# Two sparse graph-attention layers: denominators summed into rows, masks read earlier, 17 targets summed early instead of 13

## The chip, the core and the metric

The kernel runs on one core of a Trainium2 chip: TensorE (PE) for products, VectorE (DVE), ScalarE (ACT) and GpSimd (POOL) for elementwise work, and DMA queues, most of them issued by SyncE (SP) and, for gathers, by GpSimd. The metric is the device time of one execution in microseconds (us). Before the change the median of three runs is 1807.55 us (1801.66 to 1808.13).

## The reference

There are N = 3327 nodes with 1024 features, an adjacency matrix (int32, symmetric, ones on its diagonal, some 17 ones in a row), and two layers. Each adds an attention over the neighbours to its input and normalizes the sum. Everything is f32.

```
# layer 0, eight heads of 128
h     = (x @ W0).reshape(N, 8, 128)
e     = leaky_relu(a_src·h_i + a_dst·h_j, 0.2), -inf where adj == 0
x     = layernorm(x + softmax_j(e) @ h)
# layer 1, one head
h     = x @ W1
e     = leaky_relu(h_i·a1 + h_j·a2, 0.2), excluded where adj == 0
x     = layernorm(x + relu(softmax_j(e) @ h))
```

The exponential of a leaky ReLU of a sum is written as the larger of two products of exponentials, so an edge weight is `max(r_i * u_j, v_j)` with one factor r per target and head and two numbers u, v per source and head. These 16 numbers stand behind the 1024 columns of h in each row of the table `h0_d` (1040 columns in use). A softmax is a weighted sum of rows of h divided by a sum of weights, the denominator.

## The kernel before, in words

Nodes are handled as 26 tiles of 128. A tile as the rows that are summed into is called a target here. The kernel has three stages.

**Projection** (from L743 on). For each tile: load x, transpose it on TensorE (`flip`), multiply by W0 in three column cuts of eight products each (`project`, L546), copy the result out of PSUM on ScalarE (`keep`, L565) and store it to `h0_d`. Two PSUM banks take the cuts in turn. Between every second product `pace` runs other work, one step of a Python generator at a time, so the order of all queues is written out by hand:

- *Lists.* Which edges a target has is found from its rows of adj. `load_mask` reads 128 rows by a GpSimd DMA that turns int32 into bytes, into one of three buffers (L535). `clear` takes the diagonal out (GpSimd). `words` counts the ones of each half on ScalarE (L350, two passes and their accumulators), makes `deg_b` (L352) and packs the bytes to words on DVE. `ends` and `ends2` turn counts into places with a product (L366, L391) and a string of small GpSimd operations. `keys`, `columns`, `ways`, `places`, `spread`, `give`, `take` and `sources` then pick the columns of the ones (DVE), move them to their places by products (TensorE), and leave indices `idx`, target numbers `tgt` and row factors `re_d`. The generator `listing` does this for one list after the other; a mask is counted in its last step for the list four ahead, so masks are read evenly over the projection.
- *Early sums.* Sources in the first half of the nodes (tiles 0 to 12) are complete at half time. From tile 13 on, `sums_so_far` adds up what targets 0 to EARLY - 1 receive from them: EARLY is 13. Per target it gathers two blocks of 4 x 128 rows (L641), makes weights and their products with the marks of the targets (L659, L662), sums by TensorE (L671), and stores a partial row block `half_d` and partial denominators `dens`.

**Layer 0, edges** (`sparse`, class `Layer0`, driven by `pipeline`). A target has up to five blocks: 0 and 1 with sources from the first half, 2 and 3 from all nodes, and a last one of 128 places. A target that was summed early has only the last three. Each block of 4 x 128 rows is gathered by four indirect DMAs (L1033) into one of five buffers; its buffer is free again when its products are done. `weights` makes the weights in PSUM (`way`, L1109 and L1110), copies them to SBUF (L1112, ScalarE), and multiplies them into marks (L1114, DVE, 1024 columns). `sums` then multiplies 128 x 32 pieces of that by 128 x 128 pieces of the rows, so that four groups of 32 targets go to four quarters of the output (L1145). The target's own row is scaled by its weight (`own`: L1092 on ScalarE for late targets, L1088 on DVE with the partial row added for early ones) and enters by a product with the identity (L1126).

The denominator of a block is one product with the weights of four groups and eight heads as the 32 stationary columns and the marks as 128 moving columns (L1155, L1138). That gives all 32 x 128 combinations, so `finish` masks the ones that belong together (`met`, L1167, with the constant `meets`) and adds them up with a second product (L1168, with `heads`). The early sums do the same (L719, L707, L737). Then come the division, the residual, the norm, and the stores for layer 1.

`pipeline` says with `plans` how many steps of the finishing of the previous targets run after each block. Targets alternate: a late one, then an early one.

**Layer 1, edges** (class `Target`): per target the same gathers from `y_d`, products in three cuts (L1257), then the projection by W1 (L1289) and the norm.

```
            def finish(self):

                met = sbuf("met", [NG * H, P], 2)
                nc.vector.tensor_tensor(met, self.den[: NG * H, :P], meets, OP.mult)
                nc.tensor.matmul(self.den[:, P:], met, heads, start=True, stop=True)
                yield
```

Of the kernel before, what the change touches and what calls it, by code (L numbers as in the profile page):

```python
# [9 lines left out]
F32 = mybir.dt.float32  # L10
# [16 lines left out]
def kernel(  # L27
# [57 lines left out]
    EARLY = NTH  # L85
# [35 lines left out]
    cnt = const.tile([P, NT, 4], F32, name="cnt")  # L121
# [10 lines left out]
    meets = const.tile([NG * H, P], F32, name="meets")  # L132
    heads = const.tile([NG * H, H], F32, name="heads")
# [181 lines left out]
    class Edges:  # L315
# [6 lines left out]
        def __init__(self, ph, t):  # L322
            self.ph, self.t = ph, t
            self.d, self.deg, self.end2 = cnt[:, t, :2], cnt[:, t, 2:3], cnt[:, t, 3:]
# [18 lines left out]
        def words(self, ad, junk):  # L343
# [7 lines left out]
            self.deg_b = sbuf("deg_b", [P, 2], 4, dt=BF16)  # L351
            nc.scalar.activation(self.deg_b, self.d, AF.Copy)  # L352
            w = ad.bitcast(I32)
            for n in range(3):
                m = WD >> n
                half = sbuf(f"wd{n}", [P, m], 4 if n == 2 else 1, dt=I32)
# [6 lines left out]
        def ends(self, tri_b):  # L363
# [4 lines left out]
            end, off, low, high = (v[:, n : n + 2] for n in (0, 2, 4, 6))  # L368
            self.mid, self.over, self.offs = v[:, 8:10], v[:, 10:12], v[:, 12:14]
            self.more, self.mid2, self.start, self.off2 = (v[:, n : n + 1] for n in range(14, 18))  # L370
# [5 lines left out]
            nc.gpsimd.tensor_scalar(high, end, float(HG2), None, op0=OP.max)  # L376
            nc.gpsimd.tensor_tensor(self.over, high, low, OP.subtract)
            nc.gpsimd.tensor_tensor(self.more, self.over[:, :1], self.over[:, 1:], OP.add)
            nc.gpsimd.tensor_copy(self.more_b, self.more)
            nc.gpsimd.tensor_tensor(self.deg, self.d[:, :1], self.d[:, 1:], OP.add)  # L380
            nc.gpsimd.tensor_copy(self.offs, off)
            nc.gpsimd.tensor_tensor(self.offs[:, :1], off[:, :1], self.d[:, 1:], OP.subtract)
            nc.gpsimd.tensor_tensor(self.offs[:, :1], self.offs[:, :1], self.over[:, :1], OP.subtract)
            mv = self.ph.mvs[self.t % 4][:, :, : XB + 1 : XB]
            nc.gpsimd.tensor_copy(mv[:, 0, :], self.offs)
            nc.gpsimd.tensor_tensor(mv[:, 1, :], self.offs, mv[:, 0, :], OP.subtract)

        def ends2(self, all_b):
# [6 lines left out]
            nc.gpsimd.tensor_tensor(self.off2, self.start, self.d[:, 1:], OP.subtract)  # L395
            nc.gpsimd.tensor_tensor(self.off2, self.off2, self.over[:, 1:], OP.add)
# [117 lines left out]
    with ExitStack() as own, tc.manual_schedule():  # L514
        ph = Phase(own, "proj", {"A": 2, "T": 1})
        pool, bank = ph.pool, ph.bank
        part = Phase(own, "part", {})
        opening = ExitStack()
# [35 lines left out]
        def keep(t, c):  # L554
            if t not in hts:
                hts[t] = ph.sbuf("ht", [P, HW0], 3)
            ht, acc, c0 = hts[t], accs.pop((t, c)), CUTS0[c]
            m = min(CUTS0[c + 1], D) - c0
            if c == 2:
                nc.scalar.activation(sd0[:, t].rearrange("p a h -> p (a h)"), acc[:, m:], AF.Copy)  # L560
                lists[t].factors()
# [13 lines left out]
        def count(t):  # L575
            if t < NT:
                clear(t)
                lists[t].words(ads.pop(t), junk)
                if t:
                    load_mask(t + 2)  # L580

        def listing():

            for t in range(-1, NT):
                old, new = lists[t] if t >= 0 else None, lists[t + 1] if t + 1 < NT else None
                for s in range(4):
# [4 lines left out]
                    if s == 1 and 2 < t + 3 < NT:  # L591
                        lists[t + 3].ends(tri_b)
                    if s == 2 and t >= 0:
                        clear(t + 4)
                    if s == 3 and 2 < t + 3 < NT:
                        lists[t + 3].ends2(all_b)
                    yield
# [4 lines left out]
                if new:  # L602
                    new.ways()
                yield
                if old:
                    old.sources()
                    yield
                while new and t + 1 not in scored:
# [5 lines left out]
                count(t + 4)  # L614
                yield

        scored, cleared, kept, soon = set(), set(), {}, []
        steps, slots, done = listing(), [0, 0], [0]

        def pace():  # L620

            slots[0] += 1
            while done[0] * slots[1] < slots[0] * (8 * (NT + 1)):
# [5 lines left out]
        def sums_so_far():  # L629

            part.more_banks(own, "part", {"L": 1})
            src = [near[1], part.pool.tile([P, NG, HG], F32, bufs=1, name="far"), near[0]]
# [60 lines left out]
            owed = None  # L693
            for s in range(EARLY):
                acc = part.bank("L", [P, 2, 4, DH], "part")
                made = []
                for b in range(HB):
# [7 lines left out]
                    if b == 0 and owed:  # L705
# [851 lines left out]
```

## Time and profile before

| what | value |
|---|---|
| median of three runs | 1807.55 us |
| the profiled execution | 1883.75 us, span 1882.0 |
| granted TensorE clock, mean | 0.923 |
| busy: PE, PE weight load | 1637.2 us (87%), 934.7 (50%) |
| busy: DVE, ACT, POOL | 1184.3 us (63%), 514.0 (27%), 1105.5 (59%) |
| DMA | 586.89 MB, 312 GB/s in the mean |
| queue of the gathers and masks (software) | 457.74 MB, 69.9% of the 16 engines' span |
| queue of plain transfers (hardware) | 126.52 MB, 18.3% |
| projection, layer 0, layer 1 | about 0 to 585, 585 to 1190, 1190 to 1882 us |

A group line reads: source line, engine, operation, output and inputs, shapes, count; busy time and mean of one; idle time of the engine just before it and what ended that. A line of waits has the waiting engine and line, what it waited for, the total in us, how often, and the longest. "issue" is idle time for which the profile shows no cause. The profiled execution is longer than the runs of the median, so shares and durations are read from it and its sums are made against its own time.

### The profile page before, as it was taken

To read this page: it belongs to the slowest core of one execution; us is meant where nothing else is said; L and a number is where in the kernel's file an instruction comes from. 1 tells how busy PE (TensorE), PEld (TensorE's weight loads), DVE (VectorE), ACT (ScalarE), POOL (GpSimd) and SP (SyncE) were. 2 spreads that over 40 slices of the span, in tenths; PEclk is the share of its full clock that TensorE was granted. 3 is DMA by queue.
4 is the path that set the end of the run, shared out by engine and by line. 5 is a ranking of instruction groups with operands and counts; after the bars stand their busy time and mean duration, and the time that the engine had idled before them with its cause. 6 is when DMAs were issued, how large, how long until landed. Compare 5 with 4: busy or idle time off the path is not lost.

```text
span 1882.0 us, 35565 instructions
## 1 busy us (share of the span) xinstructions
PE 1637.2 (87%) x13168; PEld 934.7 (50%) x13168; DVE 1184.3 (63%) x3262; ACT 514.0 (27%) x1519; POOL 1105.5 (59%) x1580
## 2 busy tenths in 40 slices
PE   8899899999995777778677767499999999999998
PEld 4566565565663555545454544234444444444443
DVE  5799998887755777777677786334444444444343
ACT  5666554444431222222222222011111110111110
POOL 4533356666645666666666556466666666666650
PEclk9999999999996778788888877799999999999999
DMA  7566869888779999999999999799999999999990
GB/s 184 90 136 117 149 173 261 230 273 248 272 245 348 390 403 372 374 380 389 380 394 395 363 366 328 267 369 389 385 379 373 389 390 385 369 385 377 369 355 34
DMA packets 187319, 586.89 MB, mean 312 GB/s; under 512 B 36641, under 2 KB 46651, under 8 KB 187136
## 3 DMA queue, kind: packets, MB, share of 16 engines
q0 software_dynamic: 131056, 457.74, 69.9%
q1 hardware_dynamic: 55922, 126.52, 18.3%
q8 instruction: 107, 1.75, 0.4%
q14 instruction: 76, 0.62, 0.1%
q10 hardware_dynamic: 158, 0.26, 0.0%
HBM read 587.80 MB, written 51.23 MB: 340 GB/s over the span
## 4 chain that ended last, share of the span: by engine, by line
PE 64%; DVE 14%; issue 9%; ACT 5%; DMA 5%; POOL 2%; another core or an unknown queue 0%; SPq 0%; DVEq 0%; ACTq 0%; POOLq 0%
PE mm L1289 20%; PE acc L1257 14%; PE mm L546 10%; PE acc L1145 9%; PE part L671 3%; PE acc L1126 2%; PE tr L197 2%; PE acc L1134 2%; ACT junk L350 1%; ACT own L1092 1%; DVE e L1114 1%; DMA wt<-in_L_gnn_W_dram 1%; DMA src<-h_d,idx 1%; DVE top L309 1%; DVE y L1177 1%
## 5 line engine op out<-in xcount | busy, mean ns | idle before, releaser
L546 PE MATMUL mm<-wt,xT 128*128 128x347 f32 (+1 forms) x1248 | 413.6, 473 | 4.6 <-DMA wt<-in_L_gnn_W_dram 4.2
L1289 PE MATMUL mm<-wt,xT 128*128 128x512 f32 x832 | 387.9, 605 | 0.1
L1033 POOL DMA_INDIRECT src<-y_d,idx x256 | 258.8, 1011 | 145.4 <-issue 56.6
L546 PEld LDWEIGHTS mm<-wt,xT 128*128 128x128 f32 x1248 | 227.3, 193 | 122.5 <-issue 23.9
L1033 POOL DMA_INDIRECT src<-h_d,idx x184 | 200.9, 1092 | 123.3 <-PE den L1155 34.4
L1289 PEld LDWEIGHTS mm<-wt,xT 128*128 128x128 f32 x832 | 149.6, 189 | 199.5 <-issue 194.6
L1292 DVE SCALAR_TENSOR_TENSOR o<-mm,y 128x512 f32<-128x512 f32 x52 | 36.0, 692 | 336.0 <-PE mm L1289 128.0
L1145 PE MATMUL acc<-src,e 128*32 128x128 f32 x2944 | 164.9, 335 | 50.8 <-issue 49.4
L1033 POOL DMA_INDIRECT near<-y_d,idx x160 | 160.8, 1005 | 79.0 <-issue 32.6
L1033 POOL DMA_INDIRECT near<-h_d,idx x120 | 130.9, 1091 | 80.0 <-PE acc L1145 32.3
L1145 PEld LDWEIGHTS acc<-src,e 128*32 128x32 f32 x2944 | 116.0, 134 | 111.8 <-issue 92.0
L1114 DVE TENSOR_TENSOR e<-oh,way 128x1024 f32<-128x1024 f32 x104 | 127.1, 1222 | 61.2 <-ACT w L1112 39.7
L1257 PE MATMUL acc<-src,es 128*32 128x342 f32 (+1 forms) x1536 | 138.5, 464 | 24.6 <-DVE es L1248 22.0
L1145 PE MATMUL acc<-near,e 128*32 128x128 f32 x2048 | 112.5, 339 | 48.9 <-issue 35.8
L200 ACT ACTIVATE xT<-tr 128x512 f32<-128x512 f32 x104 | 62.3, 600 | 273.5 <-PE tr L197 183.7
L1145 PEld LDWEIGHTS acc<-near,e 128*32 128x32 f32 x2048 | 81.3, 136 | 90.6 <-issue 77.3
L1271 ACT ACTIVATE z<-y,ri 128x342 f32<-128x342 f32 (+1 forms) x78 | 39.5, 569 | 309.2 <-DVE ri L1267 150.1
L1112 ACT ACTIVATE w<-way 128x32 f32<-128x32 f32 x104 | 20.3, 195 | 296.6 <-DVE way L1110 166.2
L1257 PEld LDWEIGHTS acc<-src,es 128*32 128x32 f32 x1536 | 50.4, 111 | 101.6 <-issue 54.4
L641 POOL DMA_INDIRECT near<-h_d,idx x76 | 82.3, 1082 | 28.2 <-issue 20.6
L1257 PE MATMUL acc<-near,es 128*32 128x342 f32 (+1 forms) x960 | 85.5, 455 | 3.9 <-DVE z L1274 1.7
L350 ACT ACTIVATE junk<-ad 128x1664 uint8<-128x1664 uint8 x52 | 82.5, 1586 | 4.7 <-POOL ad L339 3.4
(247 smaller groups left out, 2547.7 us busy)
## 6 DMA issues: line engine op xcount, KB each, us to landing
h_d<-ht SPq DMA_DIRECT2D x26, 520.0 KB
own<-h_d SPq DMA_DIRECT2D x26, 520.0 KB
y_d<-y SPq DMA_DIRECT2D x26, 514.0 KB
y<-y_d SPq DMA_DIRECT2D x26, 514.0 KB
x<-in_x_dram SPq DMA_DIRECT2D x25, 512.0 KB
y<-in_x_dram SPq DMA_DIRECT2D x25, 512.0 KB
out_dram<-o SPq DMA_DIRECT2D x25, 512.0 KB
ad<-in_adj_dram POOLq DMA_DIRECT2D x25, 415.9 KB
```

The costliest lines, as they stand in the source:

```text
L197: nc.tensor.transpose(tr[:, k, :], src[:, (4 * g + k) * P : (4 * g + k + 1) * P], ident)
L200: nc.scalar.activation(part, tr, AF.Copy)
L350: nc.scalar.activation(junk, ad[:, n * THR : (n + 1) * THR], AF.Copy, accum_out=self.d[:, n : n + 1])
L546: nc.tensor.matmul(acc, xT[t][:, k, :], wt[:, k, CUTS0[c] : CUTS0[c + 1]], start=k == 0, stop=k == KT - 1)
L641: nc.gpsimd.indirect_dma_start(out=src[n % 3][:, g, :], out_offset=None, in_=h0_d[:THR, :], in_offset=bass.IndirectOffsetOnAxis(ap=idx[:, ...
L671: nc.tensor.matmul(acc[g * GT : (g + 1) * GT, h // 4, h % 4, :], e[:, g, h, :], vals[:, g, h, :], start=b == 0 and h % 4 == 0, stop=b == H ...
L1033: nc.gpsimd.indirect_dma_start(out=s[:, g, :w], out_offset=None, in_=table[:n, :], in_offset=bass.IndirectOffsetOnAxis(ap=idx[:, t, b * NG ...
L1114: nc.vector.tensor_tensor(e, oh.unsqueeze(2).to_broadcast([P, ng, H, wide]), wp.unsqueeze(3).to_broadcast([P, ng, H, wide]), OP.mult,)
L1145: nc.tensor.matmul(self.acc[h // 4][g * GT : (g + 1) * GT, h % 4, :], e[:, g, h, :], rowsof[:, g, h, :], start=first and h % 4 == 0, stop= ...
L1257: nc.tensor.matmul(self.acc[c][to, :m], es[:, g, :], s[:, g, CUTS[c] : CUTS[c + 1]], start=b == 0, stop=b == EB,)
L1271: nc.scalar.activation(z[:, cut], self.res[:, cut], AF.Copy, scale=ri[:, 1:2])
L1289: nc.tensor.matmul(acc, xT[:, k, :], wt1[:, k, half], start=k == 0, stop=k == KT - 1)
```

## The change

- **Early sums of 17 targets.** EARLY goes from 13 to 17. The order in layer 0 puts two or three early targets behind each late one, and two late ones at the end.
- **Denominators straight into rows.** The marks of one group (32 columns) become the stationary operand and the weights (8 columns) the moving one, four products for a block, each into its quarter of the targets' rows. `meets`, `heads`, `met` and the second product go, here and in the early sums; `finish` has one step fewer and `plans` with it.
- **Edge products ahead of copies.** In `weights` the DVE product of marks and weights is issued before ScalarE's copy of the weights, which is needed for the denominator alone, and has 8 columns for the last block.
- **Own rows and partial rows.** The own row of early targets, too, is scaled on ScalarE, after the next block's weights; the partial row enters by a second product with the identity instead of DVE's addition. The factors of all targets are made at once (`grows`).
- **Masks in the first half.** Counting is a generator of its own, one of its two steps for a mask in every third step of `pace`; `need` makes a count happen that is wanted earlier. The lists get 3/7 of their steps up to half time and the rest after it.
- **Smaller.** GpSimd's operations on places are joined, the count of a row is added up once at the end, `factors` moves into the list's steps, the h rows have two buffers instead of three (tile 0 uses `far`), and the gather buffers of the early sums are taken in an order that leaves the first blocks of layer 0 in `near`.

```diff
-    EARLY = NTH
+    EARLY = NTH + 4
...
         def count(t):
-            if t < NT:
+            counted.add(t)
+            clear(t)
+            lists[t].words(ads.pop(t), junk)
+            if t:
+                load_mask(t + 2)
+
+        def counting():
+
+            for t in range(3, NT):
                 clear(t)
-                lists[t].words(ads.pop(t), junk)
-                if t:
-                    load_mask(t + 2)
+                yield
+                count(t)
+                yield
...
-        steps, slots, done = listing(), [0, 0], [0]
+        steps, counts, slots, done = listing(), counting(), [0], [0]
+        total, turn_at = 7 * NT + 5, ((NT // 2 - 3) * 12 + 12, (NT - 3) * 12 + 8)
...
             slots[0] += 1
-            while done[0] * slots[1] < slots[0] * (8 * (NT + 1)):
+            n = slots[0]
+            if n % 3 == 0:
+                next(counts, None)
+            first = 3 * total // 7
+            if n <= turn_at[0]:
+                aim = 4 + (first - 4) * n / turn_at[0]
+            else:
+                aim = first + (total - first) * (n - turn_at[0]) / (turn_at[1] - turn_at[0])
+            while done[0] < aim:
                 done[0] += 1
                 next(steps, None)
...
-                den = ph.dd[:, P : 2 * P + H]
+                den = ph.dd[:, P : P + H]
                 for b in range(HB):
-                    nc.tensor.matmul(
-                        den[: NG * H, :P], made[b][0].rearrange("p g h -> p (g h)"),
-                        oh[:, b * NG : (b + 1) * NG, :].rearrange("p g t -> p (g t)"),
-                        start=b == 0, stop=b == HB - 1,
-                    )
+                    for g in range(NG):
+                        nc.tensor.matmul(
+                            den[g * GT : (g + 1) * GT, :], oh[:, b * NG + g, :], made[b][0][:, g, :],
+                            start=b == 0, stop=b == HB - 1,
+                        )
...
+            def scale_own(self):
+
+                h = self.h
                 for n in range(H):
                     d = slice(n * DH, (n + 1) * DH)
-                    if t < EARLY:
-                        nc.vector.scalar_tensor_tensor(
-                            h[:, d], h[:, d], es[:, n : n + 1], self.half[:, d], op0=OP.mult, op1=OP.add
-                        )
-                    else:
-                        nc.scalar.activation(h[:, d], h[:, d], AF.Copy, scale=es[:, n : n + 1])
+                    nc.scalar.activation(h[:, d], h[:, d], AF.Copy, scale=self.es[:, n : n + 1])
...
-                w = sbuf("w", [P, NG, H], 4)
-                nc.scalar.activation(w, wp if b < EB else wp.to_broadcast([P, NG, H]), AF.Copy)
                 e = sbuf("e", [P, H * P], 3).rearrange("p (g h t) -> p g h t", g=ng, h=H)
                 nc.vector.tensor_tensor(
                     e, oh.unsqueeze(2).to_broadcast([P, ng, H, wide]),
                     wp.unsqueeze(3).to_broadcast([P, ng, H, wide]), OP.mult,
                 )
+                w = sbuf("w", [P, NG, H], 4)
+                nc.scalar.activation(w[:, :ng, :], wp, AF.Copy)
...
                 if j in (1, 2):
-                    nc.tensor.matmul(
-                        self.acc[j - 1].rearrange("p h d -> p (h d)"), ident, self.h[:, (j - 1) * HALF : j * HALF],
-                        start=False, stop=False,
-                    )
+                    for rows_ in (self.h, self.half) if self.t < EARLY else (self.h,):
+                        nc.tensor.matmul(
+                            self.acc[j - 1].rearrange("p h d -> p (h d)"), ident, rows_[:, (j - 1) * HALF : j * HALF],
+                            start=False, stop=False,
+                        )
...
-                met = sbuf("met", [NG * H, P], 2)
-                nc.vector.tensor_tensor(met, self.den[: NG * H, :P], meets, OP.mult)
-                nc.tensor.matmul(self.den[:, P:], met, heads, start=True, stop=True)
-                yield
                 ri = sbuf("ri", [P, H], 2)
-                nc.vector.tensor_tensor(ri, self.den[:, P:], self.es, OP.add)
+                nc.vector.tensor_tensor(ri, self.den, self.total, OP.add)
...
-                len(Target.blocks): ((), (2, 1), (1,), (1,), (1,), (1,)),
-                len(Target.blocks) - HB: ((), (2, 1, 1), (1, 1), (1,)),
+                len(Target.blocks): ((), (2, 1), (1,), (1,), (1,), ()),
+                len(Target.blocks) - HB: ((), (2, 1), (1, 1), (1,)),
...
-        for k in range(NTH - 2):
-            order += [late[k], early[k]]
-        order += early[NTH - 2 :] + late[NTH - 2 :]
+        n = len(late) - 2
+        for k in range(n):
+            order += [late[k], *early[k * EARLY // n : (k + 1) * EARLY // n]]
+        order += late[n:]
```

## The prediction

> **What bounds the kernel now.** I read the table of busy time by stage first, because the shares of the whole page mix stages with different limits. I cut it at the start of the early sums (260 us), the end of the projection (560), and the two ends of the edge stages (600, 1190, 1230).
>
> ```profile
> 97.00:260.00 163.00, 150.81 (x684) 99.87 (x683) 148.72 (x429) 97.60 (x311) 57.42 (x261) 0.98 0.64 126
> 260.00:560.00 300.00, 281.16 (x2460) 181.94 (x2459) 231.86 (x637) 135.52 (x424) 185.98 (x387) 0.99 0.84 255
> 600.00:1190.00 590.00, 440.01 (x5724) 298.89 (x5716) 433.23 (x1119) 139.26 (x404) 366.41 (x340) 0.81 0.99 377
> 1230.00:1882.00 652.00, 640.48 (x3510) 279.13 (x3509) 276.31 (x819) 74.89 (x153) 404.49 (x401) 1.00 0.93 353
> ```
>
> Columns after the stretch and its length: PE, PE weight load, DVE, ACT, POOL, granted clock, DMA share, GB/s. The projection is bound by TensorE (151 of 163, 281 of 300), with DVE close behind in its first part. Layer 1 is TensorE at full clock and is not touched. Layer 0 (590 us) is the stage with no busy engine but with DMA at 0.99 and 377 GB/s: I take DMA as its bound. Against that stands the next view, TensorE's waits, first in 97 to 260, then in 600 to 1190.
>
> ```profile
> PE dd L366 <- ACT deg_b L352: 11.6, 8, 3.1
> ```
> ```profile
> PE acc L1145 <- issue: 82.3, 162, 3.8
> PE den L1168 <- DVE met L1167: 41.4, 14, 4.1
> PE den L1168 <- DVE e L1114: 4.0, 1, 4.0
> ```
>
> In layer 0 TensorE is busy 440, starved of issue 82 and held by the denominator's second product 45: together 567 of 590. So TensorE is nearly as full as the DMA engines, and the two must be summed separately. DVE waits only 0.3 us in all for gathered rows there, but GpSimd, which issues the gathers, waits about 130 us for TensorE to free buffers: the queue is kept full, not the consumers starved. Last, the groups that the change touches:
>
> ```profile
> L1126 PE MATMUL acc<-own,ident 128*128 128x512 f32 x104 | 80.7, 868 | 1.1 <-issue 1.1
> L350 ACT ACTIVATE junk<-ad 128x1664 uint8<-128x1664 uint8 x52 | 82.5, 1586 | 4.7 <-POOL ad L339 3.4
> L1092 ACT ACTIVATE own<-own,es 128x128 f32<-128x128 f32 x104 | 31.8, 387 | 17.6 <-DVE es L1084 16.9 <-DVE es L1083 0.7
> L1155 PE MATMUL den<-oh,w 128*32 128x128 f32 x156 | 29.3, 299 | 1.4 <-issue 1.4
> L1168 PE MATMUL den<-heads,met 32*128 32x8 f32 x52 | 12.4, 308 | 45.7 <-DVE met L1167 41.4 <-DVE e L1114 4.0 <-issue 0.2
> L1088 DVE SCALAR_TENSOR_TENSOR own<-own,es,half 128x128 f32<-128x128 f32 x104 | 28.5, 346 | 0.5
> ```
>
> An f32 matmul leaves two records, so L1126's 104 are 52 products of 1.55 us.
>
> **Early sums, 13 to 17 targets.** Each takes two blocks of four gathers out of layer 0: 32 gathers, 4096 rows. In the trace's DMA records a 4160-byte packet takes 161 ns, so 4096 x 161 / 16 engines = 41 us of DMA time leave layer 0. Four partial rows of 512 KB come back (4 x 128 x 159 ns / 16 = 5). Layer 0's packets fill 582 us of 590; after, 546. At the same share that is 554 us, a gain of 36.
>
> TensorE in layer 0, separately: 8 blocks fewer at 270 us of L1145 / 76 blocks = 3.5 us, -28; 34 new products of the partial rows at 1.55 us, +53 (37 at the 1.1 us that they take at full clock, 68 at the 2.0 at half clock, both in the chain of waits); the second product gone, -12, and its wait, -45. Then 590 - 32 = 558 if all issue starvation stays. Both limits say 554 to 558, and two limits that meet are never both reached: I take 562, a gain of 28. Bounds: 42 (starvation shrinks and DMA carries the 406 GB/s of the 650-700 us stretch for part of the stage), and 12 (neighbouring early targets want x, own and partial rows, 1.5 MB, within one block of some 12 us, and DVE then stands in line for own; the chain has one such wait of 8.4 us and one of 8.6 for a partial row).
>
> The rest of layer 0 lies beside this: on DVE 104 L1088 (28.5 us) and 26 met (7) go, and e no longer waits for ACT's copy (39 us of DVE waits); on ACT 104 more scalings at 0.387 us (40 us on an engine busy 139 of 590; they are issued behind the next block's copy, so what they could hold is only the product of own rows a block later). GpSimd sheds 32 x 1.39 us. None of these is the bound, so they are priced at nothing; were DMA not the cover, DVE's would be worth some 1.5 us a target.
>
> In the projection, four more sums cost TensorE time, which binds there. The rows for the present price of one:
>
> ```profile
> 260.00:560.00 300.00, 61.53 (x1472) 40.77 (x1472) 0.99 0.84 255
> ```
>
> These are L671's own: 1472 records are 11.5 targets, 5.35 us each. Their denominators add 6.64 us for 22 products (L719, two a target, 0.6), the second product 4.22 (L737, 0.4), and waits in front of these and of L391 13.3 (1.15): 7.5 us a target. Cross-check: 300 us hold 12.7 targets of projection, 23.7 us each, against 163/9 = 18.1 before the sums begin, which gives the same within 0.2 us once the mask waits are set apart.
>
> **Denominators straight into rows.** One product with 128 moving columns becomes four with 8. Here a rule speaks against the change. The Trainium skill, "TensorE: Matmul & The Clock Gate", Part 3, says that weight loads overlap running matmuls only when they use different row groups; these four share all rows and differ in columns. By that rule 8 loads of about 110 ns run one after the other, 0.9 us a block against L1155's 29.3/78 = 0.38: over 70 blocks of layer 0 and 34 of the sums +54 us. The trace has the same arrangement in L1145:
>
> ```profile
> 881.97 0.19 PEld L1145 LDWEIGHTS acc<-src,e 128*32 128x32 f32 x5 [0.58 <-issue]
> ```
>
> Five such loads finish in 0.19 us, and L671's 1472 fill 40.8 us, 28 ns each. By the row 8 loads cost 0.22 us. (The last block's product takes L1168's shape, 0.48 us against 0.42 now.) I take the row: 0.45 us a target in the sums, against 0.6 + 0.4 plus the waits for met, of which only the 6.9 us listed as issue (0.6 a target) remain. A sum then costs 5.35 + 0.45 + 0.6 = 6.4 us. Second half: 4 x 6.4 - 13 x 1.1 = +11; mask waits there (2.2 + 0.7) go, -3; one list falls from the first half into the second, +1. Net +9. Ends: +4 (no waits left) to +22 (each sum at today's 7.5 and DVE at its limit: 1.2 lists at 14 us and 1.3 sums at 3.75 make 21.7 of 25 us a target).
>
> **Masks in the first half.** The order of instructions shows the last of the 26 counts at about the 15th target's projection instead of the 23rd's, and each well ahead of the matmul that needs it, so the 11.6 us wait goes. In its place about 8 more masks fall into 97-260 (one in 6 steps of the pace, 18 in 9 targets, against 10 now): ACT 8 x 3.8 = +30 on 98 of 163, DVE 8 x 1.2 less one list of 14, DMA 8 x 4.7 (the mask packets fill 122 us of 16 engines for 26 masks) = 38 on a share of 0.64, making 0.87. What is queued behind two junk passes on ACT (3.2 us) is the eviction of a product, and TensorE has two banks, 5 us of cover. I give back a third: -8. Ends: -12, and +10 (every extra mask holds TensorE 2 us). The three ACT readings stay in order on one queue; GpSimd's mask issues (0.6 us) pass no gather there, since the sums have not begun. Two row buffers instead of three make an eviction wait for the store of two targets earlier, over 10 us old by then: nothing. Some three to four small GpSimd operations a list (0.2 us each) go on an engine half idle: nothing. SP issues 12 more transfers of 0.3 us in the second half, behind x loads that have a target's lead: nothing.
>
> **Ends.** One step fewer between the last layer-0 target and layer 1, -1; the exponentials taken once on ACT are 0.4 us. The final sum, its store and the branch (566 to 587) keep their form: by the steps left over, 1.3 targets of sums remain after the last projection, as now (1.25).
>
> **Sum.** -8 + 9 - 28 - 1 = -28 us on the profiled execution's 1883.75, which gives 1856. That execution is 4% above the median of 1807.55 and nothing shows where, so I move the difference over as it is: **1780**.
>
> **Rivals.**
> - Both limits of layer 0 give way fully (42) and the mask wait goes at no cost: -12 + 6 - 42 - 1 = -49, 1758. For it: the removed wait sits between two targets, when the queue runs down. Against: a second limit a few us away. Chance 0.17.
> - The gain of layer 0 is mostly eaten by early targets standing next to each other (12), and the masks win nothing: 0 + 10 - 12 - 1 = -3, about 1804. For it: TensorE's 567 of 590, and the landings of 8 us. Chance 0.20.
> - Slower: TensorE, not DMA, bounds layer 0. Its clock stays at 0.81, the 34 products cost 2.0 us (+68), and the 45 us of met waits turn into waits for issue, since the instruction count is nearly the same (-28 blocks, -12 second product): +28 there, 1807.55 - 8 + 9 + 28 - 1 = 1836. It decides once TensorE's path is above the 546 us of packets. Against: the share of 0.99, and that TensorE with fewer gaps gets more clock, not less. Chance 0.08.
> - The forecast, 1780 (its own range 1766 to 1796): 0.55.
>
> About 0.5% (9 us, 1798.5 to 1816.6) is what a measurement can tell from no change. Faster: 0.55 + 0.17 + a part of the second rival, 0.79; within: 0.13; slower: 0.08. The range runs from 1757 to 1807: the best ends of all parts to the second rival.
>
> **What would show it.** 97-260: no wait of L366 on deg_b, DMA near 0.9, same or shorter time per target. 260-560: 25 us a target, no L737. Layer 0: about 562 us at DMA 0.97 or more, no second product, clock above 0.81. Wrong if layer 0 keeps its length with the share fallen below 0.95 (TensorE or landing waits bind), if four loads of the new denominators do not overlap, or if ACT's waits reach the projection's products.

## The result and the profile after

After the change the median is 1778.99 us (1778.42 to 1782.76, four runs) against 1804.61 us (1796.26 to 1808.13) for the kernel before on the same chip: ratio 0.9873, interval 0.9852 to 0.9893. The forecast was 1780, and the gain of 25.6 us is close to the 28 that it summed. Its terms were not that good: two of them were off by 16 and 18 us, in opposite directions, and a third by 8.

One thing has to be settled before stages are compared. The profile of before (1883.75 us) and the profile of after (1778.88 us, span 1777.1) are from chips of different speed: layer 1, whose code is the same in both, takes 690.0 us in the one and 671.1 in the other. (Which chip the first profile is from is not on record; before_again below makes it likely that it is a slower one.) So the changed kernel was run again, unchanged, on a chip where layer 1 takes 689.7 us. I call that run **after_again**; it stands beside the profile of before, and the profile of **after** stands beside the experiments on chip C. First the table of busy time by stage for after_again (stretch, its length, PE, PE weight load, DVE, ACT, POOL, granted clock, DMA share, GB/s):

```profile
100.00:247.00 147.00, 145.22 (x655) 95.74 (x654) 135.12 (x383) 116.58 (x319) 58.45 (x208) 1.00 0.89 156
247.00:572.00 325.00, 297.30 (x3166) 195.29 (x3165) 252.01 (x679) 111.54 (x419) 214.70 (x381) 0.98 0.82 281
601.00:1159.00 558.00, 427.07 (x5734) 275.14 (x5730) 396.95 (x989) 167.32 (x488) 340.90 (x317) 0.85 0.99 382
```

and the same for after on its own chip:

```profile
98.00:245.00 147.00, 145.12 (x653) 95.64 (x652) 135.13 (x383) 116.46 (x319) 58.04 (x208) 1.00 0.89 157
245.00:547.00 302.00, 282.30 (x3168) 190.47 (x3167) 251.81 (x679) 111.02 (x419) 220.96 (x381) 0.99 0.87 303
575.00:1106.00 531.00, 355.39 (x5730) 258.90 (x5728) 397.30 (x988) 167.04 (x488) 339.73 (x313) 0.80 1.01 396
```

The first rows agree, 147.0 us in both: in that stage the two chips show no difference. The next two differ by 23 and 27 us for the same instructions. In layer 0, DMA is at 0.99 to 1.01 in both, as before, but at 382 and 396 GB/s, and TensorE is busy for 427 us on one chip and 355 on the other. These are the same matmuls at no lower clock (0.85 and 0.80), so the busy time of TensorE seems to contain waiting of some kind on the first chip.

The stages, cut at the first product of tile 4, of tile 13, the last of the projection, the first of layer 0 and the first of layer 1:

| us | before | after_again | difference | forecast | after |
|---|---|---|---|---|---|
| first half of the projection, tiles 4 to 12 | 162.7 | 146.9 | -15.8 | -8 | 147.0 |
| second half | 300.4 | 325.3 | +24.9 | +9 | 301.9 |
| to layer 0 | 27.0 | 28.2 | +1.2 | 0 | 27.6 |
| layer 0 and turn to layer 1 | 604.8 | 558.2 | -46.6 | -29 | 531.1 |
| layer 1 | 690.0 | 689.7 | -0.3 | 0 | 671.1 |

With 3.2 us more before tile 4 these add up to the difference of the two spans, -33.4. The medians on that chip differ by 22.3 us (1879.07 and 1856.79), so some 10 us of the table are the scatter of single executions or of chips (the execution profiled in after_again, 1850.40 us, was the fastest of its six).

The waits of TensorE in layer 0 that bear on this, from the view of after_again first, then from that of after:

```profile
PE acc L1147 <- issue: 81.0, 210, 1.1
PE acc L1130 <- ACT own L1097: 21.1, 11, 4.0
PE den L1158 <- issue: 4.4, 10, 0.6
```
```profile
PE acc L1130 <- ACT own L1097: 115.2, 24, 13.9
PE acc L1147 <- DVE e L1115: 29.8, 13, 5.0
```

L1168's 45 us of waits for `met` are gone with that product. On the slower chip the 81 us without a visible cause remain; on the faster one none is listed for these products, and TensorE waits for own rows and for weights instead. What is behind these two stands in DVE's waits of after:

```profile
DVE es L1084 <- DMA own<-h_d: 46.1, 17, 13.2
DVE way L1112 <- DMA src<-h_d,idx: 34.5, 12, 4.4
DVE way L1112 <- DMA near<-h_d,idx: 13.3, 6, 4.0
```

These are landings: on the faster chip the consumers stand at the DMA. The kernel before waited 0.3 us for gathered rows and 4.6 for own rows, but that trace is of a slower chip. There the changed kernel waits for own rows too, and little for gathered ones (after_again):

```profile
DVE es L1084 <- DMA own<-h_d: 52.8, 17, 11.9
DVE way L1112 <- DMA src<-h_d,idx: 5.4, 4, 1.9
```

So the long waits for own rows seem to have come with the change, and those for gathered rows with the faster chip. Last, the groups of after_again that answer to those shown of before:

```profile
L1130 PE MATMUL acc<-own,ident 128*128 128x512 f32 x104 | 75.0, 811 | 21.4 <-ACT own L1097 21.1 <-issue 0.3
L1130 PE MATMUL acc<-half,ident 128*128 128x512 f32 x68 | 42.6, 714 | 0.0
L1158 PE MATMUL den<-w,oh 128*32 128x8 f32 x560 | 22.8, 188 | 4.7 <-issue 4.4
L348 ACT ACTIVATE junk<-ad 128x1664 uint8<-128x1664 uint8 x52 | 82.9, 1594 | 6.2 <-POOL ad L337 4.6
L1097 ACT ACTIVATE own<-own,es 128x128 f32<-128x128 f32 x208 | 63.3, 389 | 0.0
```

The 34 products of partial rows (68 records) take 42.6 us, not 53. The new denominators of 70 blocks take 22.8 us (0.33 a block), which is less than the old 29.3 of 78.

### The profile page after: what moved, and what is told of

Read it like the earlier page. It is cut to its first block, busy times and chain, and to the rows that moved or that the text cites. A ratio compares the mean times of both kernels' runs of the same rounds, so it can differ in the third digit from the quotient of the medians.

```text
span 1777.1 us, 36731 instructions
## 1 busy us (share of the span) xinstructions
PE 1518.3 (85%) x13778; PEld 882.2 (50%) x13778; DVE 1150.6 (65%) x3125; ACT 537.5 (30%) x1602; POOL 1111.7 (63%) x1476
## 4 chain that ended last, share of the span: by engine, by line
PE 42%; DMA 18%; DVE 4%; issue 1%; ACT 1%; POOL 1%; DVEq 0%; SPq 0%; POOLq 0%; ACTq 0%
PE mm L1290 21%; PE acc L1258 13%; DMA src<-h_d,idx 7%; DMA own<-h_d 4%; PE acc L1147 3%; DMA near<-h_d,idx 3%; PE acc L1130 3%; DVE e L1115 2%; PE tr L195 1%; DMA src<-y_d,idx 1%; DMA near<-y_d,idx 1%; ACT own L1097 1%; DMA end<-h_d,idx 1%; DVE pr L1002 1%; PE acc L1138 1%
## 5 line engine op out<-in xcount | busy, mean ns | idle before, releaser
L1290 PE MATMUL mm<-wt,xT 128*128 128x512 f32 x832 | 387.6, 604 | 0.0
L1036 POOL DMA_INDIRECT src<-y_d,idx x240 | 244.6, 1019 | 95.0 <-issue 32.7
L1036 POOL DMA_INDIRECT src<-h_d,idx x168 | 180.9, 1077 | 112.4 <-PE acc L1147 25.2
L1290 PEld LDWEIGHTS mm<-wt,xT 128*128 128x128 f32 x832 | 149.7, 189 | 199.1 <-issue 194.1
L1036 POOL DMA_INDIRECT near<-y_d,idx x176 | 178.9, 1017 | 90.6 <-PE acc L1258 29.7
L1130 PE MATMUL acc<-own,ident 128*128 128x512 f32 x104 | 80.4, 865 | 118.8 <-ACT own L1097 115.2
L1120 ACT ACTIVATE w<-way 128x32 f32<-128x32 f32 (+1 forms) x96 | 18.5, 192 | 350.4 <-DVE e L1115 168.6
L1147 PE MATMUL acc<-src,e 128*32 128x128 f32 x2688 | 103.4, 318 | 17.6 <-DVE e L1115 17.6
L1258 PE MATMUL acc<-src,es 128*32 128x342 f32 (+1 forms) x1440 | 116.2, 454 | 0.2
L1258 PE MATMUL acc<-near,es 128*32 128x342 f32 (+1 forms) x1056 | 90.1, 476 | 28.0 <-DVE es L1249 28.0
L1147 PEld LDWEIGHTS acc<-src,e 128*32 128x32 f32 x2688 | 88.1, 129 | 47.1 <-DVE e L1115 31.9
L1147 PE MATMUL acc<-near,e 128*32 128x128 f32 x1792 | 65.8, 309 | 23.0 <-DVE e L1115 12.2
L1130 PEld LDWEIGHTS acc<-own,ident 128*128 128x128 f32 x104 | 20.4, 245 | 124.6 <-ACT own L1097 123.9
```

Of the source, the lines that this page charges most:

```text
L1036: nc.gpsimd.indirect_dma_start(out=s[:, g, :w], out_offset=None, in_=table[:n, :], in_offset=bass.IndirectOffsetOnAxis(ap=idx[:, t, b * NG ...
L1130: nc.tensor.matmul(self.acc[j - 1].rearrange("p h d -> p (h d)"), ident, rows_[:, (j - 1) * HALF : j * HALF], start=False, stop=False,)
L1147: nc.tensor.matmul(self.acc[h // 4][g * GT : (g + 1) * GT, h % 4, :], e[:, g, h, :], rowsof[:, g, h, :], start=first and h % 4 == 0, stop= ...
L1258: nc.tensor.matmul(self.acc[c][to, :m], es[:, g, :], s[:, g, CUTS[c] : CUTS[c + 1]], start=b == 0, stop=b == EB,)
L1290: nc.tensor.matmul(acc, xT[:, k, :], wt1[:, k, half], start=k == 0, stop=k == KT - 1)
```

## The experiments

Twelve runs on three chips. Each is compared with the kernel before on its own chip. The ratio, which has the interval, need not be that of the two medians; they differ most for masks_even (1.0069 and 1.0088). "Against after" is, on chips A and C, the ratio less that of after (0.9877 and 0.9873) times the time of before there. after itself was not run on A, so the values of A take the ratio of B. On B, where after_again ran beside the others, it is the difference of the two medians. By the intervals these values are good to some 5 us on C and 7 on A and B.

| run | chip | median, us | before there | ratio (interval) | against after, us |
|---|---|---|---|---|---|
| before_again | A | 1897.53 (one) | 1894.02 | | |
| early13 | A | 1889.23 | 1894.02 | 0.9975 (0.996 to 0.999) | +19 |
| masks_even | A | 1910.67 | 1894.02 | 1.0069 (1.005 to 1.0088) | +36 |
| old_dens | A | 1880.65 | 1894.02 | 0.9936 (0.9915 to 0.9957) | +11 |
| after_again | B | 1856.79 | 1879.07 | 0.9877 (0.9848 to 0.9906) | 0 |
| more_dma | B | 1884.91 | 1879.07 | 1.0034 (1.0019 to 1.0049) | +28 |
| more_pe | B | 1866.95 | 1879.07 | 0.9926 (0.9893 to 0.9959) | +10 |
| copy_first | B | 1853.61 | 1879.07 | 0.9865 (0.9835 to 0.9895) | -3 |
| even_list | C | 1792.97 | 1802.32 | 0.9947 (0.993 to 0.9965) | +13 |
| even_13 | C | 1800.16 | 1802.32 | 0.9989 (0.9979 to 0.9998) | +21 |
| early20 | C | 1794.96 | 1802.32 | 0.9957 (0.9941 to 0.9973) | +15 |
| half_on_dve | C | 1778.90 | 1802.32 | 0.9873 (0.9848 to 0.9898) | 0 |

**before_again and after_again: where the 4% are.** No edit.

> The kernel before, unchanged, profiled once more, because its first profiled execution (1883.75 us) lies 4% above its own runs, and the one of the changed kernel (1778.88) does not. If that execution was an odd one, the span is now near 1800 us, layer 1 takes 24.6 us a target as in the changed kernel instead of 25.2, and TensorE's 82 us of issue waits in layer 0 are mostly gone; layer 0 then takes about 570 us and is still at a DMA share of 0.99. If the profile itself costs that much in this kernel, the span is near 1880 again.

> The changed kernel, unchanged, once more, to have it, its trace and the kernel before on the same chip as the experiments: the chip of the first group of them ran the kernel before in 1894 us, with many short issue waits of TensorE, against 1804.6 in the recorded comparison. My theory expects the ratio of the record, 0.987, on such a chip too if the issue waits lie beside the DMA engines' work; if TensorE is what bounds layer 0 there, the ratio is nearer to 1 (0.993 to 1.0), because the number of TensorE's instructions is nearly the same.

The expectation for before_again failed. Its time is 1897.53 us, and its waits in layer 0 are those of the first profile:

```profile
PE acc L1145 <- issue: 89.3, 194, 3.8
PE den L1168 <- DVE met L1167: 46.1, 15, 4.1
```

On chip A, then, these waits go with the kernel's usual time (1894 us) and are no accident of one execution. The same is inferred for the first profile. On a slower chip (B) the change gives the same ratio as on the faster ones (0.9877 and 0.9873).

**more_dma and more_pe: which engine bounds layer 0.** more_dma writes 26 blocks of 512 KB to scratch memory beside the work; more_pe adds 52 products with a matrix of zeros. Neither changes a result.

```diff
+                nc.sync.dma_start(x1_d[self.t], h0_d[self.t * P : (self.t + 1) * P, :D])
```
```diff
+                    nc.tensor.matmul(
+                        self.acc[j - 1].rearrange("p h d -> p (h d)"), zero, self.h[:, (j - 1) * HALF : j * HALF],
+                        start=False, stop=False,
+                    )
```

> The changed kernel with one transfer of 512 KB between two places in DRAM added for every target of layer 0 (26 in all, nothing reads what they write). At 128 packets of 159 ns over 16 engines each takes 1.3 us of all DMA engines, 33 us in all. My theory (DMA bounds layer 0): +25 to +40 us against the changed kernel on the same chip. Rival (TensorE's own path bounds it): under +10.

> The changed kernel with two more products of zeros with the own row for every target of layer 0 (52 of 1.5 us, 78 us of TensorE time; they add nothing to the sums). My theory (TensorE has gaps that the DMA engines set): under +20 us against the changed kernel on the same chip. Rival (TensorE bounds layer 0): +50 or more.

The row of layer 0 in more_dma, then in more_pe:

```profile
601.90:1187.80 585.90, 426.57 (x5734) 279.94 (x5734) 396.84 (x988) 167.35 (x488) 333.68 (x317) 0.83 1.00 387
```
```profile
605.40:1174.10 568.70, 449.90 (x5834) 284.92 (x5834) 397.15 (x988) 167.68 (x488) 336.47 (x317) 0.90 0.98 375
```

The transfers lengthen layer 0 by 27.7 us (558.2 to 585.9) at a full DMA share and a rate of 387 instead of 382 GB/s. In the traces' DMA records the time of all packets there, spread over 16 engines, goes from 555 to 583 us: what was added is paid in full. One rival remains untried: the blocks stand ahead of the own rows on their queue, and DVE's waits for own rows go from 52.8 to 71.6 us. But if late rows alone held up the stage, its share and rate should fall, and here both rise.

The 52 products take 60.9 us by their line, yet TensorE's busy time rises by 22.8 us only. The granted clock goes from 0.85 to 0.90, and the products that were there before are shorter: those of the own rows take 66.7 us instead of 75.0, the small ones of the sums 226.4 instead of 243.6. The stage is 10.5 us longer, little more than two executions on this chip differ (551.7 us in copy_first, 558.2 in after_again). So DMA is the first limit. That TensorE is close enough behind it on this chip for 52 products not to be wholly free is likely, but not shown.

**half_on_dve: the products of the partial rows.** DVE scales the own row and adds the partial row again, for early targets.

```diff
-                    nc.scalar.activation(h[:, d], h[:, d], AF.Copy, scale=self.es[:, n : n + 1])
+                    if self.t < EARLY:
+                        nc.vector.scalar_tensor_tensor(
+                            h[:, d], h[:, d], self.es[:, n : n + 1], self.half[:, d], op0=OP.mult, op1=OP.add
+                        )
+                        continue
+                    nc.scalar.activation(h[:, d], h[:, d], AF.Copy, scale=self.es[:, n : n + 1])
...
-                    for rows_ in (self.h, self.half) if self.t < EARLY else (self.h,):
+                    for rows_ in (self.h,):
```

> The kernel after with the own row of early targets scaled and joined with the partial row on DVE again, without the 34 products with the identity. If DMA bounds layer 0 (theory), the products cost nothing and taking them away gains 0 to 4 us, and DVE's longer work loses 0 to 5: within 6 us of after (0.985 to 0.991). Rival, TensorE bounds it: 34 products of 1.5 to 2.0 us less, 25 us or more faster (below 0.976).

The time is after's, 1778.90 and 1778.99 us, with an interval of 4.5 us to either side. TensorE's busy time in layer 0 falls from 355 to 338 us and the stage goes from 531.1 to 529.7. (The products left out took 47.6 us in after. The granted clock goes from 0.80 to 0.77 and the small products of the sums, which are unchanged, take 191 us instead of 169.) The time that TensorE no longer works it waits (line numbers are the run's own: L1152 are the sums, L1135 the own rows):

```profile
PE acc L1152 <- DVE e L1120: 75.3, 26, 5.1
PE acc L1135 <- DVE own L1098: 46.9, 16, 8.7
PE acc L1135 <- ACT own L1102: 34.5, 9, 13.2
```

After waited 29.8 for `e` and 115.2 for `own`. This part of the change is worth nothing either way on this chip.

**copy_first: the order of e and the copy of the weights.** ScalarE's copy stands ahead of DVE's product again.

```diff
-                e = sbuf("e", [P, H * P], 3).rearrange("p (g h t) -> p g h t", g=ng, h=H)
...
                 w = sbuf("w", [P, NG, H], 4)
                 nc.scalar.activation(w[:, :ng, :], wp, AF.Copy)
+                e = sbuf("e", [P, H * P], 3).rearrange("p (g h t) -> p g h t", g=ng, h=H)
...
```

> The changed kernel with ScalarE's copy of the weights ahead of DVE's product of edges again. My theory (DVE's waits for the copy lie beside the DMA engines' work): +0 to +8 us against the changed kernel on the same chip. Rival (the path through DVE and ScalarE sets the pace of layer 0): +15 to +39, as far as the 39 us of such waits in the kernel before.

No difference that can be told. DVE's waits ahead of `e` do come back, 14.4 us of them for the copy and 38.5 without a visible cause, 53 in all where the kernel before had 39.7 and 14.2. They are slack, as priced.

**old_dens: denominators by `meets` and `heads` again, in both places.**

```diff
+                    nc.tensor.matmul(
+                        self.den[: NG * H, :P], self.made[n][0].rearrange("p g h -> p (g h)"),
+                        self.oh[:, n * NG : (n + 1) * NG, :].rearrange("p g t -> p (g t)"),
+                        start=n == self.blocks[0], stop=False,
+                    )
...
+                met = sbuf("met", [NG * H, P], 2)
+                nc.vector.tensor_tensor(met, self.den[: NG * H, :P], meets, OP.mult)
+                nc.tensor.matmul(self.den[:, P:], met, heads, start=True, stop=True)
+                yield
```

> The changed kernel with the denominators as before: one product of 128 moving columns a block, masking on DVE and a second product, with one more step in the finishing, in layer 0 and in the early sums. My theory (in layer 0 the waits of TensorE lie beside the DMA engines' work; in the sums each of 17 costs about 1 us more): +8 to +18, 1787 to 1797 us. Rival (the 45 us that TensorE waited for the second product in layer 0 were on the path and their end is the main gain): +25 or more, 1804 us or above.

It costs about 11 us. Layer 0 is not longer (556.5 us against 558.2, between chips A and B), though the wait is there again (L1191 is its second product, L1168 its sums):

```profile
PE acc L1168 <- issue: 66.2, 162, 2.8
PE den L1191 <- DVE met L1190: 31.9, 14, 3.8
```

These 32 us are slack beside the DMA, and waits for issue are 15 us fewer in their place. The loss seems to be in the second half of the projection, which TensorE bounds:

```profile
250.00:590.00 340.00, 309.59 (x3021) 200.47 (x3020) 252.98 (x693) 111.38 (x418) 213.27 (x380) 0.97 0.79 270
```

That and the way to layer 0 are 15 us longer than in after_again. Chip A may account for 4 of them: there the kernel before takes 4 us more in this stretch (before_again against the first profile). The place of the loss is thus inferred between two chips.

**early13 and early20: how many targets are summed early.** EARLY is NTH (13), or NTH + 7 (20) with a second step of the sums in every fifth slot of `pace`.

```diff
-    EARLY = NTH + 4
+    EARLY = NTH
```
```diff
-    EARLY = NTH + 4
+    EARLY = NTH + 7
...
             if soon:
                 next(soon[0], None)
+                if n % 5 == 0:
+                    next(soon[0], None)
```

> The changed kernel with 13 early targets instead of 17, all else kept. My theory (layer 0 is bound by DMA, the four extra sums cost TensorE some 6 us each in the projection): layer 0 is longer by 30 to 36 us, the projection shorter by 20 to 26, in all 1787 to 1793 us. Rival (the gain is that of the denominators, copies and masks, and the four sums cost what they save): 1776 to 1782.

> The kernel after with 20 early targets, an extra step of the sums in every fifth slot. If a target that is summed early is worth 9 us of layer 0 (36 us for the four, measured) and costs 5 in the projection, three more give -10 to -14 (ratio 0.980 to 0.983). If the second half has no room left, each costs 8 to 9 there and the whole stays within 5 us of after.

Four targets are worth 19 us in the whole. Layer 0 of early13:

```profile
591.50:1186.10 594.60, 451.20 (x6295) 296.93 (x6295) 407.77 (x1008) 170.40 (x497) 367.55 (x344) 0.86 0.99 380
```

That is 36.4 us more than in after_again, but on chip A, where the kernel before, too, takes 6 us more in layer 0 (610.9 in before_again, 604.8 in the first profile). So the four targets take some 30 us off, as on chip C (31.1, even_13 below). The same row shows what the rest of the change does: early13 sums as many targets early as the kernel before, yet on the same chip its layer 0 takes 594.6 us where before_again takes 610.9. The bytes are the same (226 MB), the rate is 380 instead of 371 GB/s. Some 16 us of layer 0 (one execution each) thus come from the other parts of the change. From which is not shown: old_dens, copy_first and half_on_dve take back one each and none lengthens the stage; the order of the targets and `plans` were not tried alone.

early20 was expected to gain as its first case and lost 15 us, more than its second case allowed. Layer 0 does fall, to 503.2 us, 9 a target. But up to layer 0 it takes 516.2 us from tile 4 on, where half_on_dve, whose projection is that of after, takes 473.5 on the same chip: 14 us a target, with the effect of its extra step in every fifth slot in it. The second half in early20, its stretch and its first wait of TensorE:

```profile
250.60:592.50 341.90, 303.60 (x3633) 203.97 (x3635) 263.70 (x700) 114.16 (x428) 244.44 (x404) 0.97 0.87 308
```
```profile
PE part L692 <- DVE e L683: 26.1, 14, 4.0
```

In after the same wait is 9.7 us. The sums now stand in line for DVE, which makes their `e` beside the steps of the lists. Of the three numbers tried, 17 is the best.

**masks_even, even_list and even_13: where lists and masks stand.** masks_even takes a step of the counting in every sixth slot instead of every third, so the masks go over the whole projection as before; even_list gives the lists half of their steps up to half time instead of 3/7; even_13 is even_list with 13 early targets.

```diff
-            if n % 3 == 0:
+            if n % 6 == 0:
```
```diff
-            first = 3 * total // 7
+            first = total // 2
```

> The changed kernel with one mask counted in every twelve steps of the pace instead of six, so that masks are read over the whole projection again; list pace and all else kept. My theory (early counts save TensorE some 8 to 12 us of waits on counts, and in the second half masks and gathers share the DMA engines with a few us of cost): 1785 to 1792 us. Rival (the waits were slack, or ACT's readings cost as much): 1777 to 1782.

> The kernel after, with the lists given half of their steps up to half time instead of 3/7. Open is why the projection's second half takes 325 us where 300 were measured before and 309 forecast. Theory of the pace: the list steps that the change moves behind half time (13 of 187, with their DVE and ScalarE work) are what the products wait for there, so the second half falls to 305 or less, the first half grows by at most 10, and the whole is 5 to 15 us faster than after (ratio to before 0.980 to 0.985). Rival, the sums themselves: four more sums at 4 to 5 us of TensorE each set it, the steps only change places, second half 315 or more, first half +8, whole within 4 us of after (0.986 to 0.990).

> The kernel after with even list pace and 13 early targets. Theory of the pace: without the moved steps and without the four sums the second half is as before or shorter, 285 to 303 us (it was 330 with 13 sums and 3/7), layer 0 about 582, the whole 1.5% above even_list's ratio. Rival, something else of the new listing (where factors and counts stand, two buffers of h rows) holds it: second half 320 or more, as with 3/7.

masks_even was expected to cost 6 to 13 us and cost 36. The execution profiled took 1922.54 us, 12 more than the median, so its stages are some us too long. The first half takes 157.8 us, 10.9 more than in after_again, and TensorE's wait in it is the old one:

```profile
PE dd L364 <- ACT deg_b L350: 11.1, 9, 3.5
```

In the second half, with 4/7 of the lists in it, the same wait is twice as long (it was 2.2 us there in the kernel before), and that half takes 362 us (some of it by the lower granted clock of this execution, 0.93 there against 0.98 in after_again):

```profile
PE dd L364 <- ACT deg_b L350: 22.8, 9, 4.5
```

The whole change with its lists moved behind half time but its masks left where they were is slower than the kernel before.

even_list was expected to gain and lost 13 us. Its stages:

```profile
104.50:269.00 164.50, 149.68 (x684) 98.38 (x683) 155.07 (x444) 122.34 (x347) 64.73 (x228) 0.99 0.84 143
269.00:561.70 292.70, 278.90 (x3135) 188.05 (x3134) 226.73 (x608) 103.09 (x383) 207.49 (x353) 0.99 0.88 307
```

Against half_on_dve (147.3 and 298.8 us on the same chip) the first half grows by 17.2 and the second shrinks by 6.1. The theory of the pace had 305 us or less for the second half, against the 325 of after_again. On chip C that was true without any edit (298.8), so meeting it shows nothing; what the edit itself takes off is 6.1. On the price in the first half the theory was wrong: with masks and half of the lists both in it, DVE is at 155 of 164.5 us and TensorE idles 15. The kernel before takes 162.7 us there. So early masks alone (164.5) gain nothing, fewer lists alone (157.8) a third, and only both give 147. even_13 has a second half of 280.7 us, below the 285 to 303 expected, and not the rival's 320; but both were reckoned from a slower chip (330 us in early13), so this, too, shows little. Against it the four sums of even_list cost 27.6 us up to layer 0 (459.3 to 486.9 us from tile 4 on) and give back 31.1 in layer 0 (562.2 to 531.1).

## Why the forecast held, term by term

- **Bound of layer 0: right, but the sum of the two limits was too careful and one term was left out.** It took DMA as the bound, and its DMA limit alone gave -36; it allowed for TensorE's own limit of 558 us and stopped at -28, -29 with the turn. Measured: -46.6. By the table's rates the bytes go from 604.8 x 376 = 227.4 MB to 558.2 x 382 = 213.2 MB, 14.2 less (forecast 17.0 of gathers less 2.1): at 376 GB/s that is 38 us, where the forecast had 36. The rest, 9 us, is the higher rate, which it had only in its best end (42). The runs divide it otherwise: the four targets alone take 31.1 us off on chip C, a little less than the 36. There the stage, as it is cut here, has 3516 gather packets fewer, not 4096; at their mean of 168 ns (161, which the forecast used, is the middle one) and less the 5 us of the partial rows that makes the 31. The other parts of the change take some 16 off on chip A (early13). The forecast had them "priced at nothing", because none of them is the bound. That they raise the rate of a stage bound by DMA was not foreseen, and how they do it stays open. What failed is the step "both limits say 554 to 558, and two limits that meet are never both reached": the second limit was made by adding TensorE's busy time and its waits. old_dens and half_on_dve show that this sum is no limit: 32 us of waits for `met`, or 34 products, come or go, and the stage stays within 2 us (for old_dens between two chips).
- **Denominators: the row was right.** Sixteen loads of such products, in the tile view of after (durations least, median, most; first and last start):

```profile
L1158 PEld LDWEIGHTS den<-w,oh x16: 110/112/113, 813.6 to 813.8; 128*32 128x32 f32 x16
```

  Sixteen loads of 112 ns start within 0.2 us, so they overlap each other, although they share all rows; the rule of the Trainium skill that the forecast set against the row (TensorE: Matmul & The Clock Gate, Part 3) would have made 1.8 us of them. A block costs 0.33 us on the slower chip and 12.4 us / 70 = 0.18 on the faster. The gain was put at 1.1 us for each of 17 sums, 19 us in the projection; it is 11, give or take 7, and very likely in the projection.
- **First half: right in its mechanism, half its size.** The wait for `deg_b` is gone and the DMA share is 0.89 (forecast 0.87). The term "I give back a third" for ScalarE's passes was not needed: the trace of after_again lists 0.5 us of waits for evictions there. And the fewer list steps were given next to no value in that half; with the masks early, even_list puts them at 17 us.
- **Second half: too cheap by 16 us.** "One list falls from the first half into the second, +1" is the step that failed: even_list puts it at 6 on chip C. The denominators gave some 8 less than put down. The four sums were priced at 6.4 us each; at even pace they cost 6.9 (27.6 / 4). These three make 15 of the 16 us, but they are of three chips and each is uncertain by several us, so the division is an estimate. On the slower chip the idle time by issue, too, goes from 6.9 to 15.6 us in that half. The forecast took the price of a sum as constant; beyond 17 targets early20 has it at 14 us.
- **Rivals.** TensorE as the bound of layer 0 is refuted by half_on_dve and more_pe. The crowding of own rows, feared in the second rival, does happen (46 us of DVE waits for own rows, the longest 13.2), but the DMA share of after stays at 1.01 and the stage gains more than forecast. The sign "clock above 0.81" came true on chip B (0.85) and not on the chip of the result (0.80); it did not bear on the time.
- **The 4% between profile and median.** "Nothing shows where" was a miss in part: the 82 us of issue waits were one place. It belongs to the chip, not to the kernel: the changed kernel differs by 71.5 us between the chips of after_again and after, 23 in the second half of the projection, 27 in layer 0 and 19 in layer 1.

That the total came out within 3 us is in part luck: +16 in the second half, -18 in layer 0 and -8 in the first half nearly cancel, and what is left of them, some 10 us, is no more than single executions scatter. What was not luck is the bound of layer 0, the overlap of the loads and the end of the mask wait.

## What to carry to other kernels

Where one resource is full for a whole stage, count its own bytes or work first, and expect its rate to move by a few per cent (371 to 380 GB/s here for the same bytes); another engine's busy time and waits added together are no second limit until an experiment that adds or takes away work there shows that they are. Work moved out of one stage has two prices, one in the stage that it leaves and one where it goes, and they depend on what else stands there: undoing the move of the masks alone lost 36 us here, undoing that of the lists alone 13. And before two profiles are compared, compare a stage that the change doesn't touch: 690 against 671 us in layer 1 was the sign that these two were of different chips.

## What the runs showed of the hardware

- Chips differ by 4 to 5% on this kernel: before takes 1802 to 1808 us on chip C and in the runs of the medians above, 1879 and 1894 on chips B and A. On the slower ones TensorE waits for issue among short products (81 us in layer 0 of after_again; none of it listed in after), a record of the small products of the early sums takes 40 ns of TensorE's time instead of 34 (79.2 us and 67.9 us for 1984), layer 1 takes 690 instead of 671 us, and DMA moves 382 instead of 396 GB/s in layer 0. It is not TensorE's clock: the granted clock is not lower there (0.85 and 0.80), and in layer 1 the 832 records of 128 stationary columns and 512 moving ones (L1290) take 388.0 us on the slower chip and 387.6 on the faster. The difference is in the products with 32 stationary columns (L1258 without its last block): 255 us against 225. What makes it was not tried.
- With more work for TensorE in a stage bound by DMA its granted clock was higher, 0.90 against 0.85, and 52 products that take 60.9 us added 22.8 us of busy time. With less work it was lower, 0.77 against 0.80 (half_on_dve): 34 products that took 47.6 us went and 17 us of busy time with them.
